# Layer-0 variance of a graph network from channel sums of h and h², in four column tiles of TensorE, in place of transposes and bn_stats

## The chip, the core and the metric

One core of a Trainium2 chip runs the kernel. Its engines work side by side, each through its own queue in order: TensorE (PE, with its weight loads PEld), VectorE (DVE), ScalarE (ACT), GpSimd (POOL) and SyncE (SP), which issues most of the DMAs. The metric is the device time of one execution in microseconds; less is better.

## The reference

128 graphs of 64 nodes with 128 channels each; every pair of nodes passes a message through a three-layer perceptron with two layer norms, the adjacency matrix masks the messages, their sum over j goes with the node through a second such perceptron, and the result is added to the node. Cut to what matters:

```python
def _layernorm(x, g, b):
    mu = jnp.mean(x, axis=-1, keepdims=True)
    var = jnp.mean(jnp.square(x - mu), axis=-1, keepdims=True)
    return (x - mu) * jax.lax.rsqrt(var + EPS) * g + b

def _mlp(x, w0, b0, g0, be0, w1, b1, g1, be1, w2, b2):
    h = jax.nn.relu(x @ w0 + b0)
    h = _layernorm(h, g0, be0)
    h = jax.nn.relu(h @ w1 + b1)
    h = _layernorm(h, g1, be1)
    return h @ w2 + b2

pair_feats = jnp.concatenate([f_i, f_j], axis=-1)
messages = _mlp(pair_feats, ...) * coupling_matrix[..., None]
agg = jnp.sum(messages, axis=2)
updated = part_feats + _mlp(jnp.concatenate([part_feats, agg], axis=-1), ...)
```

All inputs and the output are f32. About one pair in eight is an edge, so most messages are zero after the mask.

## The kernel before, in words

The kernel computes the messages of the edges alone. Each graph's edges are packed into 640 slots, five tiles of 128. A **chunk** is four tiles (512 slots), a **quad** is four graphs (five chunks, 20 tiles), a **block** is eight graphs (ten chunks), taken as four pairs of graphs. There are 160 chunks, 32 quads and 16 blocks. If a graph has more edges than slots, or adj is not 0 or 1, a flag computed at the end starts a dense version of everything (`dense_graph`), which these inputs don't need.

One loop runs over `n`, and in each iteration different chunks stand at different stages:

- `marks(n)`: products of edge counts (`tp`) and positions (`qs`) into the PSUM tile `mk`; DVE compares them with `cmpt` and gets the selection `s` of sending and receiving node for each slot.
- `layer0(n - 1)`: TensorE picks and adds the node terms (`abl`, `abh`, an exact split in two f32r parts) into `hps`; ACT makes `h` = relu(hps + b0), channels on partitions and edges along the row.
- `stats0(n - 2)`: the variance of `h` over its channels is needed for each edge. TensorE transposes the four tiles of `h` into the PSUM tile `hT`, and DVE takes `bn_stats` of each. After a quad's fifth chunk `std0_of` makes the standard deviation `SD`: `square_sum` joins the two halves that bn_stats gives with three operations on POOL and one on DVE, then come a step on DVE and a root on ACT.
- `layer1(n - L1)`, L1 = 9: POOL spreads `b1b` times the deviation into `sdb`; TensorE multiplies `h` with the weights `w1c`, which hold gain and centring, into `z`; DVE makes `y` = relu(z + sdb). So the division by the deviation is put off, since relu commutes with a positive factor.
- `stats1`: bn_stats of `y`, and after a quad `rstd1_of` makes the factor `Q`, with the same `square_sum`.
- `weights` and `reduce`, from iteration LW = 15 on: `w` = mask times `Q`; products of `w` and `y` summed by node into `ys`, two graphs in two column tiles of 64.

Two helpers run a step an iteration beside it: `prepare_block` for the next block (scan `rk` of adj, its counts `cum` and `deg`, the positions `pos`, then `xT` and the node terms by `w0a` and `w0b` in two column tiles) and `update_block` for the finished one (the second perceptron, with the same `std0_of` and `rstd1_of`).

A scheduler of the language sets the final order on each engine; on the chip each queue then runs strictly in that order. PSUM has eight banks: one each for `mk`, `hps`, `hT` and `ys`, two for `z`, and two (`bank()`) shared by all others. In the profile an f32 matmul shows as two instructions, one for each of its two passes.

Of the kernel before, what the change touches and what calls it, by code (L numbers as in the profile page):

```python
# [18 lines left out]
EPS = 1e-5  # L19
# [4 lines left out]
def tile_gnn(  # L24
# [36 lines left out]


    nc = tc.nc
    B, N, C = x.shape
# [11 lines left out]
    NB = NP // PB  # L76
    CPB = NCHK // NB

    xf = x.rearrange("b n c -> (b n) c")
# [17 lines left out]
    def row(ap, name, eng=nc.scalar):  # L97
# [4 lines left out]
    ones_row = const.tile([1, P], F32, name="ones_row")  # L102
    nc.vector.memset(ones_row, 1.0)
    mean_m = const.tile([P, P], F32, name="mean_m")
    nc.vector.memset(mean_m, 1.0 / C)
# [28 lines left out]
    first = const.tile([P, PB, 2, N], F32, name="first")  # L134
    nc.vector.memset(first, 1.0)
    nc.vector.memset(first[:, :, :, 0:1], 0.0)

# [20 lines left out]
    cumall = const.tile([P, NP], F32, name="cumall")  # L158
    nball = const.tile([P, NP // 8], F32, name="nball")
    W = {}  # L160
# [75 lines left out]
    def square_sum(stp, st, n, name):  # L236

        d = stp.tile([P, n], F32, name=name + "_d")
        s = stp.tile([P, n], F32, name=name + "_s")
        nc.gpsimd.tensor_tensor(d, st[:, :, 1], st[:, :, 4], op=ALU.subtract)  # L240
        nc.gpsimd.tensor_tensor(d, d, d, op=ALU.mult)  # L241
        nc.gpsimd.tensor_tensor(s, st[:, :, 2], st[:, :, 5], op=ALU.add)
        m2 = stp.tile([P, n], F32, name=name)
        nc.vector.scalar_tensor_tensor(m2, d, C / 4.0, s, op0=ALU.mult, op1=ALU.add)  # L244
        return m2

    def std0_of(stp, st, n, name):
        m2 = square_sum(stp, st, n, name)
        v = stp.tile([P, n], F32, name=name + "_v")
        nc.vector.tensor_scalar(v, m2, 1.0 / C, EPS, op0=ALU.mult, op1=ALU.add)  # L250
        sd = stp.tile([P, n], F32, name=name + "_sd")
        nc.scalar.activation(sd, v, AF.Sqrt)
        return v, sd

    def rstd1_of(stp, st, v0, n, name):
        m2 = square_sum(stp, st, n, name)
        v = stp.tile([P, n], F32, name=name + "_v")
        nc.vector.scalar_tensor_tensor(v, v0, EPS * C, m2, op0=ALU.mult, op1=ALU.add)
        sq = stp.tile([P, n], F32, name=name + "_sq")
        nc.scalar.activation(sq, v, AF.Sqrt, scale=1.0 / C)  # L260
        q = stp.tile([P, n], F32, name=name + "_q")
        nc.vector.reciprocal(q, sq)
        return q


    with ExitStack() as es:
# [4 lines left out]
        sp = es.enter_context(tc.tile_pool(name="sp", bufs=3))  # L271
        hp = es.enter_context(tc.tile_pool(name="hp", bufs=11))
        yp = es.enter_context(tc.tile_pool(name="yp", bufs=12))
# [5 lines left out]
        ps_h = es.enter_context(tc.tile_pool(name="ps_h", bufs=1, space=PSUM))  # L279
        ps_t = es.enter_context(tc.tile_pool(name="ps_t", bufs=1, space=PSUM))  # L280
        ps_z = es.enter_context(tc.tile_pool(name="ps_z", bufs=2, space=PSUM))
# [3 lines left out]
        def bank():  # L285
            return ps_m.tile([P, 512], F32, name="ms")
# [4 lines left out]
        def load_block(b):  # L291
            xn = blkp.tile([P, PB, C], F32, name="xn")
            nc.sync.dma_start(xn, xf[b * PB * P:(b + 1) * PB * P, :]
                              .rearrange("(q p) c -> p q c", p=P))
            an = blkp.tile([P, PB, N], F32, name="an")
            nc.sync.dma_start(an, adjp[:, b * PB:(b + 1) * PB, :])
            blocks[b] = {"xn": xn, "an": an}

        def prepare_block(b):
# [7 lines left out]
                out=rk.rearrange("p q j -> p (q j)"),  # L307
                data0=first[:, 0:PB // 2].rearrange("p a b j -> p (a b j)"), data1=anf,
# [5 lines left out]
            nc.vector.tensor_copy(deg, rk[:, :, N - 1])  # L314
            blk["deg"] = deg
# [22 lines left out]
            blk["qs"] = qs  # L338
            nc.vector.tensor_reduce(nball[:, b // 2:b // 2 + 1] if b % 2 else
                                    blknb, a2.rearrange("p q j -> p (q j)"),  # L340
                                    axis=AX.X, op=ALU.max, apply_absolute_value=True)
            if b % 2:
                nc.vector.tensor_tensor(nball[:, b // 2:b // 2 + 1],
                                        nball[:, b // 2:b // 2 + 1], blknb, op=ALU.max)
            yield
# [8 lines left out]
            for half in range(2):  # L354
                ps = bank()
                for k in range(4):
                    s = slice((4 * half + k) * N, (4 * half + k + 1) * N)
                    nc.tensor.matmul(ps[0:N, k * C:(k + 1) * C], lhsT=xT[:, s], rhs=w0a,  # L358
                                     start=True, stop=True)
                    nc.tensor.matmul(ps[N:P, k * C:(k + 1) * C], lhsT=xT[:, s], rhs=w0b,  # L360
                                     start=True, stop=True)

                hi = blkp.tile([P, 4, C], F32R, name="abh", bufs=6)
                lo = blkp.tile([P, 4, C], F32R, name="abl", bufs=6)
# [6 lines left out]
        blknb = const.tile([P, 1], F32, name="blknb")  # L371

# [5 lines left out]

        S, H, ST0, V0, SD, Y, ST1, Q, WT, YS = ({} for _ in range(10))

# [23 lines left out]
        def layer0(n):  # L404
# [8 lines left out]
            nc.scalar.activation(h, ps, AF.Relu, bias=b0c)  # L413
            H[n] = h

        def stats0(n):
            q, c = divmod(n, QC)
            ps = ps_t.tile([P, CH, P], F32, name="hT")
            for t in range(CH):
                nc.tensor.transpose(ps[:, t, :], H[n][:, t * P:(t + 1) * P], ident)  # L420
            if c == 0:
                ST0[q] = stp.tile([P, QT, 6], F32, name="st0")
            for t in range(CH):
                nc.vector.bn_stats(ST0[q][:, CH * c + t, :], ps[:, t, :])  # L424

        def layer1(n):
            q, c = divmod(n, QC)
            sdb = sbp.tile([P, CH, C], F32, name="sdb")
            nc.gpsimd.tensor_tensor(  # L429
                sdb, bc(W["b1b"], CH),  # L430
                SD[q][:, CH * c:CH * c + CH].unsqueeze(2).to_broadcast([P, CH, C]), op=ALU.mult)
            ps = ps_z.tile([P, CH, C], F32, name="z")
# [119 lines left out]

        L0, LS, L1 = 1, 2, QC + 4
        LW = L1 + QC + 1
# [10 lines left out]
        for n in range(end):  # L565
# [6 lines left out]
            if 0 <= n - L0 < NCHK:  # L572
                layer0(n - L0)
            if 0 <= n - LS < NCHK:
                stats0(n - LS)
                if (n - LS) % QC == QC - 1:
                    q = (n - LS) // QC
                    V0[q], SD[q] = std0_of(stp, ST0.pop(q), QT, "m20")
            if 0 <= n - L1 < NCHK:
                layer1(n - L1)  # L580
                stats1(n - L1)
                if (n - L1) % QC == QC - 1:
                    q = (n - L1) // QC
                    Q[q] = rstd1_of(stp, ST1.pop(q), V0.pop(q), QT, "m21")
            q, c = divmod(n - LW, QC)
# [15 lines left out]

        fl = const.tile([P, 2], F32, name="fl")
        nc.vector.tensor_reduce(fl[:, 0:1], cumall, axis=AX.X, op=ALU.max)
# [3 lines left out]
        ps = bank()  # L607
        nc.tensor.transpose(ps[0:2, 0:P], fl, ident)
        f2 = const.tile([2, 1], F32, name="f2")
        nc.vector.tensor_reduce(f2, ps[0:2, 0:P], axis=AX.X, op=ALU.max)  # L610
        ps = bank()
        nc.tensor.matmul(ps[0:1, 0:1], lhsT=f2, rhs=mean_m[0:2, 0:1], start=True, stop=True)
        flag = const.tile([1, 1], I32, name="flag")
# [122 lines left out]

    over = nc.values_load(flag[0:1, 0:1], min_val=0, max_val=2)
    with tc.If(over > 0):
# [36 lines left out]
```

## Time and profile before

| | |
|---|---|
| Median of 3 runs | 771.95 us (771.48 to 772.86) |
| Profiled execution | 771.45 us, span 769.7 us |
| ScalarE: relu of layer 0 | 160 of 688 ns |
| VectorE: bn_stats of layer 0 / of layer 1 | 640 of 283 ns / 640 of 278 ns |
| VectorE: s, y | 160 of 684 ns, 160 of 676 ns |
| TensorE: transposes of h | 640 of 288 ns |

A row of the profile names the line of the kernel, the engine, the operation, the tiles as out<-in, the shapes and the count, then busy time in us, the mean length of one in ns, and the engine's idle time before these with what ended most of it. The rows of a timeline begin with the start and the length in us. Lengths overlap: an engine begins the next instruction before the last is through, so the time that an instruction holds its queue is read from the starts of two neighbours.

### The profile page before, as it was taken

The page shows a single profiled execution, that of the slowest core. Times are in us where ns is not written, and L with a number is a line of the kernel's source. Part 1 is how long each engine was busy: PE and PEld are TensorE (multiplying, and loading weights), DVE is VectorE, ACT ScalarE, POOL GpSimd, SP SyncE. Part 2 cuts the span into 40 slices and gives each one's busy share as a digit, 9 for nine tenths or more (in the row PEclk, how much of TensorE's full clock was granted, in tenths as well). Part 3 has the DMA queues.
Part 4 walks back from the last instruction along what each step waited for, and adds up shares of the span by engine and source line. Part 5 has one row for each costly group of instructions (what it writes and reads, how often), then busy time and mean ns, then how long its engine had stood idle before and what let it go on. Part 6 is the DMA issues. An engine that isn't in the chain of part 4 may idle for free.

```text
span 769.7 us, 15357 instructions
## 1 busy us (share of the span) xinstructions
PE 654.7 (85%) x5667; PEld 558.6 (73%) x5667; DVE 673.4 (87%) x2397; ACT 208.0 (27%) x402; POOL 366.1 (48%) x651
## 2 busy tenths in 40 slices
PE   2688899898898979889898988889799898989773
PEld 2567778687777868778786877778687787878663
DVE  7678998988888999898998989989989898999872
ACT  1143232232232223223322323222232233222111
POOL 6346345444354454545455454545545354435531
PEclk9699999999899999999999999989999999999997
DMA  5000000100001010000101000010000000000000
GB/s 137 1 21 8 3 8 1 35 1 24 12 2 36 1 30 7 15 22 1 35 3 35 1 17 14 1 29 1 29 1 16 1 1 14 1 15 2 14 15 16
DMA packets 27883, 12.04 MB, mean 16 GB/s; under 512 B 10391, under 2 KB 27805, under 8 KB 27805
## 3 DMA queue, kind: packets, MB, share of 16 engines
q1 hardware_dynamic: 26496, 11.01, 5.1%
q8 instruction: 46, 0.75, 0.4%
q14 instruction: 33, 0.26, 0.1%
q10 hardware_dynamic: 1308, 0.01, 0.1%
HBM read 6.82 MB, written 4.19 MB: 14 GB/s over the span
## 4 chain that ended last, share of the span: by engine, by line
PE 48%; DVE 36%; POOL 10%; issue 2%; ACT 2%; DMA 1%; ACTq 0%; POOLq 0%; DVEq 0%
PE z L435 8%; PE ys L476 7%; DVE st L446 7%; PE ms L504 7%; PE hps L410 7%; DVE s L401 7%; PE hT L420 5%; DVE st L424 5%; PE mk L396 4%; PE ms L358 3%; DVE y L234 3%; POOL xo L488 3%; PE ms L494 2%; DVE uo L538 2%; POOL sdb L429 2%
## 5 line engine op out<-in xcount | busy, mean ns | idle before, releaser
L429 POOL TENSOR_TENSOR sdb<-b1b,m_sd 128x512 f32<-128x512 f32 x160 | 168.1, 1052 | 194.4 <-DVE y L234 136.0
L435 PE MATMUL z<-w1c,h 128*128 128x128 f32 x1280 | 201.3, 288 | 2.9 <-DVE y L234 2.5
L413 ACT ACTIVATE h<-hps,b0c 128x512 f32<-128x512 f32 x160 | 110.1, 688 | 311.8 <-PE hps L410 308.4
L435 PEld LDWEIGHTS z<-w1c,h 128*128 128x128 f32 x1280 | 173.4, 197 | 16.0 <-DVE y L234 7.6
L424 DVE BATCH_NORM_STATS2 st<-hT 128x6 f32<-128x128 f32 x640 | 147.4, 283 | 4.1 <-PE hT L420 3.9
L446 DVE BATCH_NORM_STATS2 st<-y 128x6 f32<-128x128 f32 x640 | 137.4, 278 | 0.0
L401 DVE TENSOR_TENSOR s<-mk,cmpt 128x512 fp32r<-128x512 f32 x160 | 109.4, 684 | 15.9 <-PE mk L396 14.8
L410 PE MATMUL hps<-s,abl 128*128 128x512 f32 (+3 forms) x256 | 101.9, 408 | 18.1 <-DVE s L401 17.7
L420 PE MATMUL hT<-ident,h 128*128 128x128 f32 x640 | 104.8, 288 | 6.6 <-DVE st L424 6.2
L234 DVE CUSTOM_DVE_ANT_0 y<-z,sdb 128x512 f32<-128x512 f32 x160 | 107.9, 676 | 1.3 <-POOL sdb L429 1.3
L396 PE MATMUL mk<-tp,qs 128*128 128x512 f16 (+3 forms) x256 | 66.4, 312 | 38.6 <-DVE s L401 30.1
L420 PEld LDWEIGHTS hT<-ident,h 128*128 128x128 f32 x640 | 75.2, 146 | 24.3 <-DVE st L424 18.7
L476 PE MATMUL ys<-y,w 128*64 128x128 f32 x1280 | 91.0, 281 | 1.8 <-DVE w L461 1.8
L476 PEld LDWEIGHTS ys<-y,w 128*64 128x64 f32 x1280 | 73.2, 139 | 14.9 <-issue 10.2
L410 PE MATMUL hps<-s,abh 128*128 128x512 f32 (+3 forms) x256 | 81.8, 336 | 0.0
L410 PEld LDWEIGHTS hps<-s,abl 128*128 128x128 f32 x256 | 51.6, 202 | 26.8 <-DVE s L401 20.2
L396 PEld LDWEIGHTS <-qs 128*128 128x128 f16 x256 | 25.1, 100 | 58.8 <-issue 57.0
L461 DVE TENSOR_TENSOR w<-ms,m_q 128x512 f32<-128x512 f32 (+1 forms) x128 | 61.0, 479 | 0.4 <-PE ms L456 0.4
L410 PEld LDWEIGHTS hps<-s,abh 128*128 128x128 f32 x256 | 52.0, 203 | 0.9
L240 POOL TENSOR_TENSOR m_d<-st 128x20 f32<-128x20 f32 x64 | 15.9, 248 | 73.8 <-DVE st L424 52.1
L244 DVE SCALAR_TENSOR_TENSOR m<-m_d,m_s 128x20 f32<-128x20 f32 x64 | 11.5, 179 | 32.0 <-POOL m_d L241 29.9
L488 POOL TENSOR_TENSOR xo<-xn,cu2b 128x512 f32<-128x512 f32 x16 | 20.5, 1282 | 34.3 <-DVE uo L538 33.3
(162 smaller groups left out, 939.1 us busy)
## 6 DMA issues: line engine op xcount, KB each, us to landing
xn<-in_x_dram SPq DMA_DIRECT2D x16, 256.0 KB, 2.8
out_dram<-uo SPq DMA_DIRECT2D x16, 256.0 KB, 2.3
an<-in_adj_dram SPq DMA_DIRECT2D x16, 128.0 KB, 2.2
w<-in_L_gnn_msg_w_dram SPq DMA_DIRECT2D x2, 64.0 KB, 2.3
u<-in_L_gnn_upd_w_dram SPq DMA_DIRECT2D x2, 64.0 KB, 2.1
w0a<-in_L_gnn_msg_w_dram SPq DMA_DIRECT2D x1, 64.0 KB, 1.8
w0b<-in_L_gnn_msg_w_dram SPq DMA_DIRECT2D x1, 64.0 KB, 2.4
u0a<-in_L_gnn_upd_w_dram SPq DMA_DIRECT2D x1, 64.0 KB, 2.3
```

The lines of the kernel that those rows point to most:

```text
L234: nc.vector._custom_dve(TENSOR_ADD_SAT, out=o, in0=ps, in1=sb, s0=BIG, s1=0.0)
L396: nc.tensor.matmul(ps[:, at:at + w], lhsT=blocks[g // (2 * PB)]["qs"][:, g // 2 % PB, g % 2, :], rhs=TP[g // 2][:, e:e + w], start=True, s ...
L401: nc.vector.tensor_tensor(s, ps, cmpt[:, o:o + CH * P], op=ALU.is_equal)
L410: nc.tensor.matmul(ps[:, at:at + w], lhsT=ab[:, g % 4, :], rhs=s[:, at:at + w], start=(k == 0), stop=(k == 1))
L413: nc.scalar.activation(h, ps, AF.Relu, bias=b0c)
L420: nc.tensor.transpose(ps[:, t, :], H[n][:, t * P:(t + 1) * P], ident)
L424: nc.vector.bn_stats(ST0[q][:, CH * c + t, :], ps[:, t, :])
L429: nc.gpsimd.tensor_tensor(sdb, bc(W["b1b"], CH), SD[q][:, CH * c:CH * c + CH].unsqueeze(2).to_broadcast([P, CH, C]), op=ALU.mult)
L435: nc.tensor.matmul(ps[:, t, :], lhsT=h[:, t * P:(t + 1) * P], rhs=W["w1c"], start=True, stop=True)
L446: nc.vector.bn_stats(ST1[q][:, CH * c + t, :], Y[n][:, t, :])
L461: nc.vector.tensor_tensor(w[:, t0:t1], ps[:, 0:nt * P].rearrange("p (t g m) -> p t g m", t=nt, g=2), qv[:, t0:t1].unsqueeze(3).to_broadcas ...
L476: nc.tensor.matmul(YS[b][g * N:(g + 1) * N, k, :], lhsT=w[:, t, g, :], rhs=y, start=(t == 0), stop=(t == TG - 1))
```

## The change

The layer-0 variance is computed as mean(h²) - mean(h)². ACT also squares `h` into `h2`. On every second chunk `sums(n)` has four products on TensorE: `h` and `h2` of this chunk and of the one before, each against `rowsel`, a 128x32 matrix that has 1/128 in one column and zeros elsewhere. Each product writes its own 32 partitions of one PSUM bank, `sm`, so the four stand in the four column tiles of 32. Two such groups add up in one bank. After four chunks (a batch, SB = 4) ACT copies the bank out (`sums_out`), TensorE transposes it in four pieces (`stats0(b)`), and DVE copies the means out, squares, subtracts; ACT takes the root.

Besides: the three small operations of `square_sum` go from POOL to DVE; EPS goes into the bias of the roots; `deg` and `cum` are copied by ACT and not by DVE; `nball` has a column for each block; `cmpt` is f16; `h` has 10 buffers instead of 11, `an` 3 instead of 5, the node terms 5 instead of 6; L1 is 8 instead of 9; and the flag at the end also asks whether the subtraction may have lost accuracy (mean² more than 16 times the variance).

```diff
+    rowsel = const.tile([P, 2, 32], F32, name="rowsel")
+    nc.vector.memset(rowsel, 0.0)
+    for r in range(2):
+        nc.vector.memset(rowsel[:, r, r:r + 1], 1.0 / C)
...
-    cmpt = const.tile([P, 4 * CAP], F32, name="cmpt")
+    cmpt = const.tile([P, 4 * CAP], F16, name="cmpt")
...
-        nc.gpsimd.tensor_tensor(d, st[:, :, 1], st[:, :, 4], op=ALU.subtract)
-        nc.gpsimd.tensor_tensor(d, d, d, op=ALU.mult)
-        nc.gpsimd.tensor_tensor(s, st[:, :, 2], st[:, :, 5], op=ALU.add)
+        nc.vector.tensor_tensor(d, st[:, :, 1], st[:, :, 4], op=ALU.subtract)
+        nc.vector.tensor_tensor(s, st[:, :, 2], st[:, :, 5], op=ALU.add)
+        nc.vector.tensor_tensor(d, d, d, op=ALU.mult)
...
-            nc.vector.tensor_copy(cum, ps[:, 0:PB])
+            nc.scalar.copy(cum, ps[:, 0:PB])
             deg = blkp.tile([P, PB], F32, name="deg", bufs=5)
-            nc.vector.tensor_copy(deg, rk[:, :, N - 1])
+            nc.scalar.copy(deg, rk[:, :, N - 1])
...
             nc.scalar.activation(h, ps, AF.Relu, bias=b0c)
             H[n] = h
-
-        def stats0(n):
-            q, c = divmod(n, QC)
-            ps = ps_t.tile([P, CH, P], F32, name="hT")
+            h2 = h2p.tile([P, CH * P], F32, name="h2")
+            nc.scalar.activation(h2, h, AF.Square)
+            H2[n] = h2
+
+        def sums(n):
+
+            b, c = divmod(n - 1, SB)
+            if c == 0:
+                SM[b] = ps_s.tile([P, CH * P], F32, name="sm")
+            for k, src in enumerate((H[n - 1], H2.pop(n - 1), H[n], H2.pop(n))):
+                nc.tensor.matmul(SM[b][32 * k:32 * k + 32, :], lhsT=rowsel[:, c // 2, :], rhs=src,
+                                 start=(c == 0), stop=(c == SB - 2))
+
+        def sums_out(b):
+            t = smp.tile([P, CH * P], F32, name="sums")
+            nc.scalar.copy(t, SM.pop(b))
+            SM[b] = t
+
+        def stats0(b):
+
+            src = SM.pop(b)
+            ps = bank()
             for t in range(CH):
-                nc.tensor.transpose(ps[:, t, :], H[n][:, t * P:(t + 1) * P], ident)
-            if c == 0:
-                ST0[q] = stp.tile([P, QT, 6], F32, name="st0")
-            for t in range(CH):
-                nc.vector.bn_stats(ST0[q][:, CH * c + t, :], ps[:, t, :])
+                nc.tensor.transpose(ps[:, t * P:(t + 1) * P], src[:, t * P:(t + 1) * P], ident)
+
+            v = ps.rearrange("p (t o k r) -> p k r o t", t=CH, o=2, k=2)
+            mm = stp.tile([P, 2, SB // 2, 2, CH], F32, name="mm")
+            for k in range(2):
+                nc.vector.tensor_copy(mm[:, k], v[:, k, 0:SB // 2])
+            mf = mm.rearrange("p k r o t -> p k (r o t)")
+            s = slice(b * SB * CH, (b + 1) * SB * CH)
+            nc.vector.tensor_tensor(msq[:, s], mf[:, 0], mf[:, 0], op=ALU.mult)
+            nc.vector.tensor_tensor(var0[:, s], mf[:, 1], msq[:, s], op=ALU.subtract)
+            sd = stp.tile([P, SB * CH], F32, name="sd")
+            nc.scalar.activation(sd, var0[:, s], AF.Sqrt, bias=eps_c)
+            SD[b] = sd
...
-        L0, LS, L1 = 1, 2, QC + 4
+        L0, LS, LT = 1, 2, 3
+        L1 = LT + SB + 1
...
-            if 0 <= n - LS < NCHK:
-                stats0(n - LS)
-                if (n - LS) % QC == QC - 1:
-                    q = (n - LS) // QC
-                    V0[q], SD[q] = std0_of(stp, ST0.pop(q), QT, "m20")
+            if 0 <= n - LS < NCHK and (n - LS) % 2:
+                sums(n - LS)
+                if (n - LS) % SB == SB - 1:
+                    sums_out((n - LS) // SB)
+            if 0 <= n - LT < NCHK and (n - LT) % SB == SB - 1:
+                stats0((n - LT) // SB)
```

The scheduler places the new operations. On TensorE before, in the middle of the program, the four transposes of a chunk (hT) stand between its layer 0 (hps) and an older chunk's layer 1 (z):

```order
L410 MATMUL hps<-s,abl 128x512
L410 MATMUL hps<-s,abh 128x512
L420 MATMUL hT<-ident,h 128x128 x4
L435 MATMUL z<-w1c,h 128x128 x2
L396 LDWEIGHTS qs
L396 MATMUL mk<-tp,qs 128x512
L435 MATMUL z<-w1c,h 128x128 x2
```

On TensorE now, a group of sums that stayed whole, on every second chunk (32x512 is its output; the inputs are h and h2 of two chunks):

```order
L420 MATMUL hps<-s,abl 128x384
L420 MATMUL hps<-s,abh 128x384
L420 MATMUL hps<-s,abl 128x128
L420 MATMUL hps<-s,abh 128x128
L435 MATMUL sm<-h,rowsel 32x512
L435 MATMUL sm<-h_2064,rowsel 32x512
L435 MATMUL sm<-h,rowsel 32x512
L435 MATMUL sm<-h_2132,rowsel 32x512
L471 MATMUL z<-w1c,h 128x128 x4
```

Four full-width transposes are gone from each chunk, and four products 32 wide stand there on every second one. In 47 of the 80 groups they stand so. In the other 33 the first product is torn off, as here on TensorE a little earlier, by transposes of the update (uh):

```order
L420 MATMUL hps<-s,abl 128x384
L420 MATMUL hps<-s,abh 128x384
L435 MATMUL sm<-h,rowsel 32x512
L530 MATMUL ms<-ident,uh 128x128 x4
L435 MATMUL sm<-h_1937,rowsel 32x512
L435 MATMUL sm<-h,rowsel 32x512
L435 MATMUL sm<-h_2007,rowsel 32x512
L471 MATMUL z<-w1c,h 128x128 x4
L512 MATMUL ys<-y,w 64x128 x10
```

So a full-width matmul now stands between two narrow stretches. Over the whole program (the dense version in it) TensorE goes between full-width and narrow outputs, or between widths of 64 and 32, 373 times, where it was 201.

On VectorE before, in an iteration with an update, ISA is the custom operation that makes y or uh, and m and um are small statistics that come from POOL:

```order
L244 SCALAR_TENSOR_TENSOR m_2714<-m_d,m_s 128x20
L376 TENSOR_SCALAR tp<-slot,cumall 128x640
L250 TENSOR_SCALAR m_v<-m_2714 128x20
L446 BN_STATS st_2602<-y 128x6 x4
L234 ISA uh<-ms,m_2622 128x512
L401 TENSOR_TENSOR s<-mk,cmpt 128x512
L511 BN_STATS ust_2755<-uh 128x6 x4
L424 BN_STATS st_2779<-hT 128x6 x4
L234 ISA y<-z,sdb 128x512
```

On VectorE now, around the four small operations of a batch (mm, msq, var) and the three that came from POOL (m_d, m_s, m_d):

```order
L453 COPY mm<-ms 128x16 x2
L456 TENSOR_TENSOR msq<-mm 128x16
L248 ISA y<-z,sdb 128x512
L457 TENSOR_TENSOR var_148<-mm,msq 128x16
L386 TENSOR_SCALAR tp<-slot,cumall 128x640
L482 BN_STATS st_2155<-y 128x6 x4
L411 TENSOR_TENSOR s<-mk,cmpt 128x512
L254 TENSOR_TENSOR m_d<-st_2155 128x20
L255 TENSOR_TENSOR m_s<-st_2155 128x20
L386 TENSOR_SCALAR tp<-slot,cumall 128x640
L256 TENSOR_TENSOR m_d<-m_d 128x20
```

The layer-0 bn_stats are gone from the queue, and the small statistics no longer leave it for POOL.

More of the change, by code (lines that the diff above doesn't have):

```diff
@@ L133, in tile_gnn @@
     nc.vector.memset(cmpt[0:N, :], 1.0)
-    first = const.tile([P, PB, 2, N], F32, name="first")
+    first = const.tile([P, PB, N], F32, name="first")
     nc.vector.memset(first, 1.0)
-    nc.vector.memset(first[:, :, :, 0:1], 0.0)
+    nc.vector.memset(first[:, :, 0:1], 0.0)
     w0a = mat(mw0[0:C, :], "w0a")
@@ L158, in tile_gnn @@
     cumall = const.tile([P, NP], F32, name="cumall")
-    nball = const.tile([P, NP // 8], F32, name="nball")
+    nball = const.tile([P, NB], F32, name="nball")
+    msq = const.tile([P, NCHK * CH], F32, name="msq")
+    var0 = const.tile([P, NCHK * CH], F32, name="var0")
     W = {}
@@ L377, in make_tp @@
             TP[p] = tp
-        S, H, ST0, V0, SD, Y, ST1, Q, WT, YS = ({} for _ in range(10))
+        S, H, H2, SM, SD, Y, ST1, Q, WT, YS = ({} for _ in range(10))
         def pieces(n):
@@ L607, in tile_gnn @@
         ps = bank()
-        nc.tensor.transpose(ps[0:2, 0:P], fl, ident)
-        f2 = const.tile([2, 1], F32, name="f2")
-        nc.vector.tensor_reduce(f2, ps[0:2, 0:P], axis=AX.X, op=ALU.max)
+        nc.tensor.transpose(ps[0:4, 0:P], fl, ident)
+        f2 = const.tile([4, 1], F32, name="f2")
+        nc.vector.tensor_reduce(f2, ps[0:4, 0:P], axis=AX.X, op=ALU.max)
         ps = bank()
-        nc.tensor.matmul(ps[0:1, 0:1], lhsT=f2, rhs=mean_m[0:2, 0:1], start=True, stop=True)
+        nc.tensor.matmul(ps[0:1, 0:1], lhsT=f2, rhs=mean_m[0:4, 0:1], start=True, stop=True)
         flag = const.tile([1, 1], I32, name="flag")
```

53 lines of the change are left out of this document (29 added, 24 removed).

## The prediction

> **What bounds the kernel now.** The page comes first, then the same engines in the steady part.
>
> ```profile
> span 769.7 us, 15357 instructions
> PE 654.7 (85%) x5667; PEld 558.6 (73%) x5667; DVE 673.4 (87%) x2397; ACT 208.0 (27%) x402; POOL 366.1 (48%) x651
> ```
>
> VectorE and TensorE are both nearly full, which the shares alone don't rank. So I cut the run into stages. The 16 blocks (four graph pairs, ten chunks each) are marked by one matmul, L333, that runs once a block:
>
> ```profile
> 107.06 0.60 PE L333 MATMUL ms<-pos,dq 128*128 128x256 f32 x2
> ...
> 648.02 0.60 PE L333 MATMUL ms<-pos,dq 128*128 128x256 f32 x2
> ```
>
> Twelve blocks lie between, so the period is (648.02 - 107.06) / 12 = 45.1 us. The busy times of just that stretch (columns: length, then PE, PEld, DVE, ACT, POOL, then the granted clock), and below it two shorter pieces of it:
>
> ```profile
> 107.06:648.02 540.96, 481.32 (x4226) 413.83 (x4225) 491.32 (x1771) 154.05 (x300) 264.55 (x467) 0.96 0.05 14
> 188.66:233.00 44.34, 39.12 (x328) 33.28 (x325) 38.14 (x138) 12.83 (x25) 20.57 (x38) 0.92 0.06 16
> 277.30:321.60 44.30, 39.08 (x355) 33.23 (x354) 41.28 (x151) 12.89 (x26) 22.65 (x40) 1.00 0.06 16
> ```
>
> Per block: DVE 40.9 us, PE 40.1, POOL 22.0, ACT 12.8, of 45.1. Which of the two waits for the other is told by the waits of the same stretch (us in all, times, longest):
>
> ```profile
> DVE m L244 <- POOL m_d L241: 24.5, 37, 1.2
> PE mk L396 <- DVE s L401: 23.9, 34, 0.8
> PE hps L410 <- DVE s L401: 16.5, 12, 1.5
> DVE s L401 <- PE mk L396: 12.0, 7, 2.9
> PE mk L396 <- DVE tp L376: 6.8, 12, 0.6
> ```
>
> PE waits for DVE in 47.2 us of these rows; DVE waits for PE in 12.0. DVE's largest wait is for POOL: the small statistics go DVE, POOL, DVE, and DVE stands still for 24.5 / 12 = 2.0 us a block. So DVE sets the end, with PE only 0.8 us a block less busy. Whatever is taken from DVE and put on PE meets that second limit at once.
>
> **DVE, part by part.** The change takes away the layer-0 bn_stats (st<-hT) and adds small operations.
>
> ```profile
> 352.73 0.88 DVE L424 BATCH_NORM_STATS2 st<-hT 128x6 f32<-128x128 f32 x4
> 353.52 0.68 DVE L234 CUSTOM_DVE_ANT_0 y<-z,sdb 128x512 f32<-128x512 f32 x1
> ```
>
> Four of them hold the queue from 352.73 to 353.52, 0.79 us (0.88 is their overlapping length). Ten chunks a block: -7.9.
>
> ```profile
> L314 DVE COPY deg<-rk 128x4 f32<-128x4 f32 x16 | 10.3, 644 | 0.0
> L244 DVE SCALAR_TENSOR_TENSOR m<-m_d,m_s 128x20 f32<-128x20 f32 x64 | 11.5, 179 | 32.0 <-POOL m_d L241 29.9
> L244 DVE SCALAR_TENSOR_TENSOR um<-um_d,um_s 128x4 f32<-128x4 f32 x32 | 5.0, 156 | 2.1 <-POOL um_d L241 2.1
> ```
>
> The deg copy goes to ACT: -0.6. Two layer-0 small operations on each of two quads go: 4 x 0.18 = -0.7. New are, a block, 6 operations for the two layer-1 quads, 6 for the update and 10 for 2.5 batches of layer-0 sums (two copies, a product, a subtraction). No row shows these; the nearest are 0.156 and 0.179 us, and the deg row (0.644, a four-element copy) is the far end. I take 0.16, so 22 x 0.16 = +3.5; at 0.644 it would be +14.2. Sum: -5.7, so DVE needs 35.2 us a block, and the 2.0 us of waiting for POOL goes with the POOL steps. Only at the far end (45.9) would DVE still bind. What is late next is PE.
>
> **PE, part by part**, over the whole run.
>
> ```profile
> L420 PE MATMUL hT<-ident,h 128*128 128x128 f32 x640 | 104.8, 288 | 6.6 <-DVE st L424 6.2
> 353.97 0.60 PE L420 MATMUL hT<-ident,h 128*128 128x128 f32 x4
> 354.41 0.83 PE L435 MATMUL z<-w1c,h 128*128 128x128 f32 x6
> 355.08 0.60 PE L494 MATMUL ms<-ident,uh 128*128 128x128 f32 x4
> 355.61 1.31 PE L476 MATMUL ys<-y,w 128*64 128x128 f32 x20
> 356.85 1.16 PE L504 MATMUL ms<-u1c,uhT 128*128 128x128 f32 x8
> 357.85 0.38 PE L396 MATMUL mk<-tp,qs 128*128 128x512 f16 x1
> ```
>
> Transposes: four start at 353.97 and the next matmul at 354.41, so 0.11 each. 640 go (-70.4); 40 batches bring 4 each (+17.6).
>
> The 80 groups of column-sum products. An f32 product is two passes (the count of two a product in L333), and a pass of 256 columns takes 0.60 - 0.38 = 0.22 us:
>
> ```profile
> L333 PE MATMUL ms<-pos,dq x32: 379/382/794, 14.5 to 648.2; 128*128 128x256 f32 x32
> ```
>
> So 512 columns are 0.44 a pass, 0.87 us a product alone. Do four column tiles run at once? The trace has two:
>
> ```profile
> 345.60 0.32 PE L358 MATMUL ms<-w0a,xT 128*64 128x128 f32 x1
> 345.61 0.32 PE L360 MATMUL ms<-w0b,xT 128*64 128x128 f32 x1
> 345.76 0.27 PE L358 MATMUL ms<-w0a,xT 128*64 128x128 f32 x1
> 345.77 0.27 PE L360 MATMUL ms<-w0b,xT 128*64 128x128 f32 x1
> ...
> 346.42 0.27 PE L358 MATMUL ms<-w0a,xT 128*64 128x128 f32 x1
> 346.42 0.27 PE L360 MATMUL ms<-w0b,xT 128*64 128x128 f32 x1
> ```
>
> Two different streams start together and the pair repeats every 0.11, the time of one full-width pass: two tiles cost what one does. Four are not shown. Bounds for a group: 0.44 (were a narrow pass to stream at twice the rate) to 3.48 (one after another). I take 0.87, four at once, since the nearest row overlaps fully: 80 x 0.87 = +69.6.
>
> In the program's order 33 of the 80 groups are torn: the first product stands alone, then other matmuls, then the other three. The lone one overlaps nothing: +33 x 0.87 = +28.7.
>
> Every change between full-width and narrow matmuls costs. Above, the transposes from 355.08 should end at 355.52 but ys starts at 355.61 (0.09); ys's ten pairs need 1.09 of 1.24 (0.15); u1c's eight passes need 0.89 of 1.00 (0.11). That is 0.35 for a round trip. The order has 373 changes after and 201 before, 86 round trips more: +30.
>
> Sum for PE: -70.4 + 17.6 + 69.6 + 28.7 + 30 = +75.5 us, 4.7 a block. PE goes from 40.1 to 44.8, DVE from 40.9 to 35.2: the bound moves to PE, at about the old period.
>
> The Trainium skill, "TensorE: Matmul & The Clock Gate", section "Part 3: Packing small matmuls — row/col tiling", gives 2.38 times for three column tiles of 512 columns, not 3; at that efficiency a group would take 1.26 times a lone product, an estimate, +18 us in all and 775 us in place of 757. The two-tile rows show no such loss, and no run here shows three or four.
>
> **Hidden parts.** ACT gains a square a chunk and a copy of the sums every four:
>
> ```profile
> L413 ACT ACTIVATE h<-hps,b0c 128x512 f32<-128x512 f32 x160 | 110.1, 688 | 311.8 <-PE hps L410 308.4
> L429 POOL TENSOR_TENSOR sdb<-b1b,m_sd 128x512 f32<-128x512 f32 x160 | 168.1, 1052 | 194.4 <-DVE y L234 136.0
> ```
>
> At 0.69 each, 12.5 a block are 8.6; ACT goes to 21.4 of 45 and waits for PE's layer 0 most of its time, so this costs nothing while a square ends within the iteration between its layer 0 and its sums. Were that cover gone, each fourth product would wait up to 0.69, 80 x 0.69 = 55 us. POOL loses small steps and its sdb is unchanged. The layer-0 deviations now have two iterations (9 us) before their use instead of three; sums copy 0.69, four transposes 0.60, four DVE steps 0.64 and one sdb 1.05 are 3.0 and a root, so some 6 us are left for queueing. The pipeline is one iteration shorter, worth 0 to 4.5 us at the end; I take 2.
>
> **The sum.** Per block: 44.8 for PE. Off this goes part of the slow clock: it stands at 0.96, and a mean of 0.04 below full is 0.04 x 45 = 1.8 us; a piece at 0.92 and one at 1.00 stand above with like work. These dips need idle PE, and I let half go (-0.9). On it come PE's waits that stay: of 47.2 / 12 = 3.9 us I keep a tenth, 0.4, because DVE now has 9 us to spare. Period 44.3, and 16 x (45.1 - 44.3) = 12.8 less, with the shorter end 14.8. The profiled execution took 771.45 us (span 769.7), so 756.7; the median of the runs is 0.5 higher: 757.
>
> **Rivals.**
> 1. More gain: PE never starves, so clock dips and waits both go: 44.8 - 1.8 = 43.0, less the pipeline tails after each wait inside "busy" (0.27 us long less the 0.11 it holds the queue, 0.16, times five), 42.2: 46 us less, 725. For it: PE's idle time is nearly all DVE's doing. Against: 640 transposes are replaced by work in which PE still depends on single PSUM banks. The skill's same page, section "Part 4: PE-mode transpose", says transposes don't count as activity for the clock; by that rule the dips would go with them and this rival's 725 is the time. The piece at 1.00 above ran with all its transposes, which does not bear it out. Chance 0.10.
> 2. Slower, by PE's in-order queue: the place is the 33 torn groups and their switches, which make PE full; it decides from 0.3 us of waiting a block (44.8 + 0.3 = 45.1) if the clock stays at 0.96. With 1.5 us, a third of today's: 46.3, +19, 790. Chance 0.20.
> 3. The products overlap only two at a time: each of 80 groups takes 0.87 more, +70: 827. Chance 0.13. One after another: 47 whole groups x 3 and 33 torn ones x 2 are 207 x 0.87 = +180: 937. Chance 0.04. Here the change doesn't do what its four tiles say.
> 4. Both limits meet and nothing moves: 0.06.
>
> **Chances.** The forecast (742 to 768) has 0.47. Faster by over 0.2%, the least that this kernel's runs can tell from no change: 0.47 + 0.10 = 0.57; within it 0.06; slower 0.20 + 0.13 + 0.04 = 0.37. The range reaches from just above rival 1 to rival 3: 730 to 828.
>
> **What would show it.** Right: sm products in fours that start within 0.05 us and hold PE about 0.9; PE busier than DVE; DVE's rows of waiting for POOL's m_d gone; DVE rows of waiting for PE (s for mk, y for z) grown to several us a block. Wrong: a stagger of 0.4 or more inside a whole group (rival 3); PE's clock unchanged with PE waiting over 1 us a block for DVE, ACT or sdb (rival 2); new two-input DVE steps far above 0.16.

## The result, and the profile after

The changed kernel takes 743.36 us (median of 4 runs, 741.81 to 745.39) against 771.92 us before: 0.963 times the time, 95% interval 0.960 to 0.966. It is 28.6 us faster, where 15 were forecast; 743.36 lies in the range of 730 to 828, near the fast end of the forecast (742 to 768), 13.6 us below the predicted 757.

The page of the changed kernel, first the span and the busy times, then the chain that ended last (here by engine):

```profile
span 743.3 us, 15105 instructions
PE 678.8 (91%) x5827; PEld 504.9 (68%) x5827; DVE 619.9 (83%) x1998; ACT 335.3 (45%) x642; POOL 311.5 (42%) x363
...
PE 54%; DVE 33%; POOL 5%; DMA 3%; issue 2%; ACT 1%; SPq 0%; DVEq 0%; ACTq 0%; POOLq 0%
```

PE and DVE have changed places: PE is now the fuller one. Its share of the chain was 48% before and is 54% now, so the chain alone doesn't tell that the limit moved. The same block marker as before (now L349), from the timeline of PE:

```profile
95.97 0.70 PE L349 MATMUL ms<-pos,dq 128*128 128x256 f32 x2
...
618.05 0.70 PE L349 MATMUL ms<-pos,dq 128*128 128x256 f32 x2
```

That is (618.05 - 95.97) / 12 = 43.5 us a block, 1.57 less than before. The busy times of these twelve blocks and of the two pieces ahead of them (length, then PE, PEld, DVE, ACT, POOL, granted clock):

```profile
95.97:618.05 522.08, 498.93 (x4346) 372.29 (x4345) 451.96 (x1464) 248.84 (x479) 225.75 (x254) 0.99 0.05 15
...
0.00:58.00 58.00, 39.73 (x258) 26.27 (x259) 38.64 (x95) 24.47 (x46) 29.85 (x51) 1.00 0.20 49
58.00:95.97 37.97, 36.02 (x327) 26.39 (x325) 32.52 (x105) 19.18 (x36) 16.22 (x22) 1.00 0.02 5
```

The same of the kernel before, at its start:

```profile
0.00:58.00 58.00, 35.24 (x210) 28.04 (x210) 40.69 (x102) 13.85 (x22) 28.57 (x52) 0.85 0.21 53
58.00:107.06 49.06, 41.82 (x353) 34.75 (x352) 44.98 (x164) 13.00 (x24) 24.18 (x44) 1.00 0.02 4
```

The span is 26.4 us shorter, and the markers say where: twelve blocks at 1.57 are 18.9 us; the fourth block's marker comes 11.1 us earlier (95.97 against 107.06), with the clock at 1.00 in the first 58 us instead of 0.85; and the end behind the last marker is 3.6 us longer (125.3 against 121.7). Per block PE is busy 41.6 us, DVE 37.7, ACT 20.7, POOL 18.8.

The waits of the twelve blocks (us in all, times, longest):

```profile
DVE y L248 <- PE z L471: 33.9, 31, 1.4
DVE abl L379 <- ACT abh L378: 20.6, 23, 2.1
...
PE mk L406 <- DVE s L411: 9.7, 17, 1.1
...
DVE uh L248 <- PE ms L540: 8.0, 12, 0.7
```

DVE's waits for POOL (m_d) are gone, PE's waits for `s` have shrunk from 23.9 and 16.5 us to 9.7, and DVE now waits for PE's `z`.

The groups of four products, from PE's timeline, one whole (eight instructions are four products of two passes) and one torn:

```profile
309.00 0.39 PE L420 MATMUL hps<-s,abh 128*128 128x512 f32 x1
309.32 1.06 PE L435 MATMUL sm<-h,rowsel 128*32 128x512 f32 x8
310.31 1.16 PE L471 MATMUL z<-w1c,h 128*128 128x128 f32 x8
311.31 0.44 PE L492 MATMUL ms<-pick,tp 128*128 128x128 f16 x5
...
323.13 1.05 PE L435 MATMUL sm<-h,rowsel 128*32 128x512 f32 x2
324.11 0.32 PE L370 MATMUL ms<-w0a,xT 128*64 128x128 f32 x1
...
325.72 1.06 PE L435 MATMUL sm<-h,rowsel 128*32 128x512 f32 x6
326.71 1.16 PE L471 MATMUL z<-w1c,h 128*128 128x128 f32 x8
```

Read from start to start: four products together hold PE for 0.99 us, one alone for 0.98, three for 0.99. So the four column tiles run at once, and a torn group costs twice what a whole one does. Over the run 47 groups are whole (median 0.996) and 33 torn (0.976 and 0.989), as the order showed.

The full-width neighbours of a group pay too. In the kernel before, the same two stand beside each other:

```profile
339.25 0.40 PE L410 MATMUL hps<-s,abh 128*128 128x512 f32 x1
339.49 1.05 PE L435 MATMUL z<-w1c,h 128*128 128x128 f32 x8
340.38 0.28 PE L456 MATMUL ms<-pick,tp 128*128 128x128 f16 x2
```

There hps holds PE 0.24 us and eight passes of z 0.89. Around a group it is 0.32 (309.00 to 309.32) and 1.00 (310.31 to 311.31). With the 0.12 by which a group's 0.99 exceeds the 0.87 of one product alone, a round trip between the widths costs some 0.3 us.

DVE's small operations by shape, of the whole run (count, then busy us, mean ns):

```profile
L456 DVE TENSOR_TENSOR msq<-mm 128x16 f32<-128x16 f32 x40 | 23.2, 580 | 0.0
...
L255 DVE TENSOR_TENSOR m_s<-st 128x20 f32<-128x20 f32 x32 | 16.3, 510 | 0.0
...
L254 DVE TENSOR_TENSOR um_d<-ust 128x4 f32<-128x4 f32 x32 | 11.7, 366 | 0.1
...
L457 DVE TENSOR_TENSOR var<-mm,msq 128x16 f32<-128x16 f32 x40 | 6.5, 162 | 0.0
```

The last row is what was expected of all of them; the first three are two to four times that. All nine new groups come to 101 us, 6.3 a block instead of 3.5.

### The profile page after: what moved, and what is told of

Same layout as the page of the kernel before. It is cut to its first block, busy times and chain, and to the rows that moved or that the text cites. A ratio compares the mean times of both kernels' runs of the same rounds, so it can differ in the third digit from the quotient of the medians.

```text
span 743.3 us, 15105 instructions
## 1 busy us (share of the span) xinstructions
PE 678.8 (91%) x5827; PEld 504.9 (68%) x5827; DVE 619.9 (83%) x1998; ACT 335.3 (45%) x642; POOL 311.5 (42%) x363
## 4 chain that ended last, share of the span: by engine, by line
PE 54%; DVE 33%; POOL 5%; DMA 3%; issue 2%; ACT 1%; SPq 0%; DVEq 0%; ACTq 0%; POOLq 0%
PE z L471 10%; PE sm L435 10%; PE ms L540 8%; PE ys L512 7%; DVE y L248 6%; PE hps L420 6%; DVE st L482 5%; DVE s L411 5%; PE ms L370 4%; PE mk L406 3%; PE ms L530 3%; DVE w L497 3%; DMA an<-in_adj_dram 2%; POOL sdb L465 2%; DVE ust L547 2%
## 5 line engine op out<-in xcount | busy, mean ns | idle before, releaser
L465 POOL TENSOR_TENSOR sdb<-b1b,sd 128x512 f32<-128x512 f32 x160 | 166.3, 1052 | 158.9 <-ACT sd L459 83.4
L471 PEld LDWEIGHTS z<-w1c,h 128*128 128x128 f32 x1280 | 159.9, 191 | 69.7 <-issue 64.7
L471 PE MATMUL z<-w1c,h 128*128 128x128 f32 x1280 | 182.9, 282 | 2.6 <-DVE y L248 2.6
L248 DVE CUSTOM_DVE_ANT_0 y<-z,sdb 128x512 f32<-128x512 f32 x160 | 108.9, 681 | 46.5 <-PE z L471 44.3
L435 PE MATMUL sm<-h,rowsel 128*32 128x512 f32 x640 | 121.3, 607 | 0.0
L426 ACT ACTIVATE h<-h 128x512 f32<-128x512 f32 x160 | 100.7, 629 | 4.0
L512 PE MATMUL ys<-y,w 128*64 128x128 f32 x1280 | 84.7, 279 | 0.7 <-DVE w L497 0.7
L520 POOL TENSOR_TENSOR m<-c2u,deg 128x512 f32<-128x512 f32 x16 | 16.6, 1040 | 98.8 <-DVE uh L248 89.8
L378 ACT CAST abh<-ms 128x512 fp32r<-128x512 f32 x32 | 18.7, 585 | 55.5 <-PE ms L372 55.5
L379 DVE TENSOR_TENSOR abl<-ms,abh 128x512 fp32r<-128x512 f32 x32 | 22.1, 691 | 24.0 <-ACT abh L378 23.7
L370 PEld LDWEIGHTS ms<-w0a,xT 128*64 128x64 f32 x256 | 29.9, 144 | 15.1 <-DVE w L497 11.7
```

The lines of the kernel that those rows point to most:

```text
L248: nc.vector._custom_dve(TENSOR_ADD_SAT, out=o, in0=ps, in1=sb, s0=BIG, s1=0.0)
L426: nc.scalar.activation(h2, h, AF.Square)
L435: nc.tensor.matmul(SM[b][32 * k:32 * k + 32, :], lhsT=rowsel[:, c // 2, :], rhs=src, start=(c == 0), stop=(c == SB - 2))
L465: nc.gpsimd.tensor_tensor(sdb, bc(W["b1b"], CH), SD[b][:, CH * c:CH * c + CH].unsqueeze(2).to_broadcast([P, CH, C]), op=ALU.mult)
L471: nc.tensor.matmul(ps[:, t, :], lhsT=h[:, t * P:(t + 1) * P], rhs=W["w1c"], start=True, stop=True)
L512: nc.tensor.matmul(YS[b][g * N:(g + 1) * N, k, :], lhsT=w[:, t, g, :], rhs=y, start=(t == 0), stop=(t == TG - 1))
```

## The experiments

**The theory** after the result: before, DVE set the pace (its work and its wait for POOL), and PE's busy time overstated what PE needed; the change takes DVE's work away, so PE's torn groups become the next thing that costs. **Rivals:** the gain comes from the small statistics that left POOL; or PE had been the limit all along and gained by the clock; or a torn group is hidden anyway.

### 1 and 2. The small statistics alone, and the change without them

In the kernel before, the three operations of `square_sum` go to VectorE (first run); in the changed kernel they go back to POOL (second run, the same edit the other way):

```diff
-        nc.gpsimd.tensor_tensor(d, st[:, :, 1], st[:, :, 4], op=ALU.subtract)
-        nc.gpsimd.tensor_tensor(d, d, d, op=ALU.mult)
-        nc.gpsimd.tensor_tensor(s, st[:, :, 2], st[:, :, 5], op=ALU.add)
+        nc.vector.tensor_tensor(d, st[:, :, 1], st[:, :, 4], op=ALU.subtract)
+        nc.vector.tensor_tensor(s, st[:, :, 2], st[:, :, 5], op=ALU.add)
+        nc.vector.tensor_tensor(d, d, d, op=ALU.mult)
```

> The kernel before, with only the three small statistics operations of square_sum moved from POOL to DVE (six places a block, so 18 operations). My theory (DVE sets the end before, and the gain of the change is the bn_stats that leave it): DVE loses 2.0 us a block of waiting for POOL and gains 18 x 0.16 = 2.9 us of work, so about +0.9 us a block: 772 to 790 us, granted clock still near 0.956. Rival (the gain comes mainly from ending the handoffs between DVE and POOL): 745 to 760 us.

> The changed kernel, with only the small statistics put back on POOL. My theory (PE sets the end after, DVE has 5.8 us a block to spare): the handoffs return to DVE's queue but fall into its slack, 742 to 750 us. Rival (handoffs matter): 2.0 us a block or more come back, 775 us or more.

Measured: 797.97 us, 1.034 times before (1.030 to 1.038), and 742.5 us, 0.961 (0.957 to 0.965), the changed kernel's own time. The windows of the first between its markers:

```profile
111.10:672.10 561.00, 500.74 (x4226) 430.34 (x4225) 515.49 (x1982) 153.99 (x300) 224.53 (x251) 0.92 0.05 13
```

The first run is slower than its theory's 772 to 790 us, and its clock fell to 0.92 where 0.956 was expected; the rival, a gain, is out. DVE goes to 515.49 / 12 = 43.0 us a block, 2.1 more than before, and the period to 46.75, 1.7 more. That fits DVE as the limit, with a wait for POOL that was cheaper than the work done by itself; alone it doesn't prove it, since PE's busy time also grew, by 1.6 us a block at the lower clock. In the second run, whose time the theory forecast, the wait is back:

```profile
DVE y L248 <- PE z L471: 24.3, 19, 1.5
...
DVE m L258 <- POOL m_d L255: 21.4, 18, 2.1
```

It is 21.4 us in place of part of the waiting for `z`, and the time is the same. In the changed kernel this part brought nothing: the 2.0 us a block of DVE's waiting that the prediction saw go were no gain. The other small changes that came along (`cmpt` in f16, fewer buffers, L1 = 8) were not tried apart; `s`, which reads `cmpt`, takes 680 ns where it took 684.

### 3. The groups kept whole by a critical section

The loop of the four products moves in under the section, otherwise unchanged:

```diff
+            with tc.tile_critical():
                 for k, src in enumerate((H[n - 1], H2.pop(n - 1), H[n], H2.pop(n))):
```

> The changed kernel, with the four products of a group kept together in PE's order (no group is torn; before 33 of 80 were). A lone product held PE 0.98 us with its switches. My theory (PE sets the end): 33 x 0.98 = 32 us less work on PE; most of it is gained, 712 to 724 us. Rival (DVE, busy 37.7 of 43.5 us a block, is the next limit close by, or PE's waits take its place): 733 us or more.

Measured: 796.89 us, 1.031 (1.027 to 1.035). A miss. The theory's 712 to 724 us did not come. All 80 groups are whole, but a row of the waits in its profiled execution (810 us) shows what the section costs:

```profile
PEld sm L436 <- issue: 95.3, 81, 3.0
```

Ahead of a group's weight load the queue of loads stands 95.3 / 81 = 1.2 us with nothing to wait for that the profile shows, and PE itself is idle ahead of each of the 80 groups for 1.0 us on the mean, 80 us in all, where 33 lone products of 0.98 were to be saved. So the run says nothing on the theory; run 5 reaches the same order without a section.

### 4. The square done twice on ACT

```diff
             nc.scalar.activation(h2, h, AF.Square)
+            nc.scalar.activation(h2, h, AF.Square)
```

> The changed kernel, with ACT's square of h done twice (the second overwrites the first): 160 x 0.63 = 101 us more on ACT, 27 of 43.5 us a block. My theory (ACT is covered): 742 to 750 us. Rival (PE waits for the squares, or the longer ACT queue delays the relu that frees the layer-0 bank): 0.63 us on every second chunk or more, 790 us or more.

Measured: 743.95 us, 0.965 (0.960 to 0.970), the changed kernel's time, with ACT at 26.5 us a block. As forecast, ACT's part is hidden, with room for one more square a chunk.

### 5. The four products written in the reverse order

```diff
-            for k, src in enumerate((H[n - 1], H2.pop(n - 1), H[n], H2.pop(n))):
+            for k, src in reversed(list(enumerate((H[n - 1], H2.pop(n - 1), H[n], H2.pop(n))))):
```

The product that is ready last (`h2` of this chunk) now stands first, so the scheduler has nothing to start early.

> The changed kernel, with the four products of a group written in the reverse order, so that the scheduler tears none of the 80 groups (33 were torn) and PE changes its width 309 times and not 373; nothing drains PE and no wait is added, as the section of e3 did. My theory (PE sets the end; a lone product holds it 0.98 us with its switches): 33 x 0.98 = 32 us less on PE, 712 to 726 us. Rival (DVE, 37.7 of 43.5 us a block, or a chain through ACT and POOL is the limit close by): 733 us or more.

Measured: 710.31 us, 0.921 (0.915 to 0.926), 33 us below the changed kernel. All 80 groups are whole in its trace. Its windows:

```profile
89.47:587.11 497.64, 469.90 (x4346) 368.49 (x4344) 450.90 (x1464) 247.16 (x479) 226.92 (x254) 1.00 0.06 16
```

PE is busy 39.2 us a block instead of 41.6, and the period is 41.5 instead of 43.5. A group that stays whole saves a lone product's 0.98 us and what its switches cost the neighbours, some 0.2: 33 x 1.17 = 39 us, which is also about what PE's busy time fell by (16 x 2.4 us). The gain is 33 us, a little more than was forecast: most of the loss of a torn group is paid, and it was in the result all the time. DVE's waits for `z` fall with it, from 33.9 us in the twelve blocks to 11.

### 6 and 7. The whole groups with a load on PE, and with one on DVE

Two of the four layer-1 products of each chunk are done twice (320 products of two passes of 0.11 us, 71 us, 4.4 a block); or two of its bn_stats (64 us, 4.0 a block):

```diff
-            for t in range(CH):
+            for t in (0, 0, 1, 1, 2, 3):
                 nc.tensor.matmul(ps[:, t, :], lhsT=h[:, t * P:(t + 1) * P], rhs=W["w1c"],
```

```diff
+            for t in range(2):
+                nc.vector.bn_stats(ST1[q][:, CH * c + t, :], Y[n][:, t, :])
```

> The kernel of e5 with two of the four layer-1 products of each chunk done twice: 160 x 4 passes x 0.11 = 71 us more on PE, all groups still whole. My theory (PE sets the end after the change): 55 us or more above e5. Rival (PE has room, something else sets the end): under 30 us above e5.

> The kernel of e5 with two more bn_stats of y a chunk (written over the same statistics): 320 x 0.2 = 64 us more on DVE (7 of 80 groups are torn in its order, 7 us). My theory (DVE has over 4 us a block to spare): under 35 us above e5, of which 7 are torn groups. Rival (DVE still sets the end): 60 us or more above e5.

Measured: 751.95 us (0.975, 0.968 to 0.982), 42 more than run 5 for 71 us of PE's work; and 745.8 us (0.967, 0.959 to 0.974), 35.5 more for 64 us of DVE's. In run 7 seven groups are torn again, some 7 of the 35.5 us. So each load costs about half of itself (42 of 71; 28 of 64), and neither theory's number came. The likely reading is that PE and DVE share the limit; each load also gives the scheduler another order, and that was not held apart.

### 8. The same PE load in the kernel before

> The kernel before with the same load on PE as in e6 (71 us of products). My theory (before, DVE sets the end and PE idles 5.0 us a block): 16 x 4.5 = 71 us of work fall mostly into 80 us of idle time, 780 to 805 us. Rival (PE set the end before already): 830 us or more.

Measured: 771.17 us against 771.14, ratio 1.003 (0.999 to 1.008). 71 us of work on PE cost nothing that can be told from zero, less than the theory's 780 to 805 us allowed. Its windows:

```profile
106.63:642.87 536.24, 504.19 (x4706) 452.69 (x4705) 489.35 (x1766) 151.57 (x300) 264.03 (x467) 1.00 0.05 14
```

PE's busy time grows by 1.9 us a block (42.0 against 40.1) for 4.4 of work, and the granted clock of the stretch goes from 0.96 to 1.00. PE was not the limit before: with its gaps filled, it needs at most 42.0 - 4.4 = 37.6 us a block, not 40.1. At most, because PE is still idle 2.7 us of a block in this run, so some of what counts as busy is waiting yet.

### 9. The same PE load in the changed kernel

> The changed kernel (32 of its groups torn) with the load of e6 on PE: two of four layer-1 products of each chunk done twice, 71 us of PE. Before, this load cost nothing (e8); in the kernel with whole groups 42 us (e6). My theory (in the changed kernel PE, busy 41.6 of 43.5 us a block, sets the end alone): 55 us or more above it, 798 us or more. Rival (DVE and PE share the limit there as in e6): 780 to 792 us.

Measured: 781.27 us, 1.009 (1.007 to 1.012), 38 more than the changed kernel, in the rival's range. (Runs 9 to 12 were made on another chip, where the kernel before took 773.64 us and not 771.14; by the ratios it is 36 more.) The load now costs about half of itself, where it was free before. The windows:

```profile
98.59:649.13 550.54, 543.15 (x4827) 424.54 (x4825) 453.24 (x1464) 250.45 (x480) 225.96 (x254) 1.00 0.05 14
```

PE is busy 45.3 of 45.9 us. Less the load, the changed kernel needs at most 40.9 us of PE a block, 3.3 more than run 8's 37.6 (both at a clock of 1.00). The 3.3 are the least that the change added, since PE is full here and was not in run 8. The remaining 2.6 of the changed kernel's 43.5 are gaps that the load first fills.

### 10. All products of the sums in one column tile

Each of the eight products of a batch has a selector with its column elsewhere, and all write partitions 0 to 31 (cut to the products; the copy and the transposes behind them take these 32 partitions alone):

```diff
-                nc.tensor.matmul(SM[b][32 * k:32 * k + 32, :], lhsT=rowsel[:, c // 2, :], rhs=src,
-                                 start=(c == 0), stop=(c == SB - 2))
+                nc.tensor.matmul(SM[b][0:32, :], lhsT=rowsel[:, 2 * k + c // 2, :], rhs=src,
+                                 start=(c == 0 and k == 0), stop=(c == SB - 2 and k == 3))
```

> The changed kernel with all products of the sums in one column tile (each source its own row of the same 32 partitions, one after another), so none overlaps. My theory (four tiles run at once, a group holds PE 0.87 us and not 3.5): 47 whole groups lose 3 x 0.87 and 33 torn ones 2 x 0.87, 180 us in all, 900 to 935 us. Rival (the tiles save little, since the streams share something, or PE has room): 800 us or less.

Measured: 884.65 us, 1.144 (1.140 to 1.148), 141 more than the changed kernel. PE's timeline has a lone product and its three others:

```profile
329.80 1.04 PE L435 MATMUL sm<-h,rowsel 128*32 128x512 f32 x2
...
332.38 2.76 PE L435 MATMUL sm<-h,rowsel 128*32 128x512 f32 x6
335.08 1.16 PE L473 MATMUL z<-w1c,h 128*128 128x128 f32 x8
```

Three products hold PE for 2.70 us (332.38 to 335.08) instead of 0.99, and a whole group 3.55 (median) instead of 0.996. The overlap of the column tiles is what makes the change pay; without it the kernel is slower than before by 111 us. The 141 fall short of the forecast 180 in two steps. PE is busy 10.2 us a block more (51.75 in the window between its markers, against 41.58), 163 us in all; and 1.7 of these fill gaps that the changed kernel had, so the period is 8.4 longer.

### 11 and 12. The whole groups with the small statistics on POOL

Run 5 with `square_sum` on POOL, as in run 2; then with `msq` and `var` there as well:

```diff
-            nc.vector.tensor_tensor(msq[:, s], mf[:, 0], mf[:, 0], op=ALU.mult)
-            nc.vector.tensor_tensor(var0[:, s], mf[:, 1], msq[:, s], op=ALU.subtract)
+            nc.gpsimd.tensor_tensor(msq[:, s], mf[:, 0], mf[:, 0], op=ALU.mult)
+            nc.gpsimd.tensor_tensor(var0[:, s], mf[:, 1], msq[:, s], op=ALU.subtract)
```

> The kernel of e5 (whole groups) with the three operations of square_sum back on POOL. DVE's two-input small operations take 0.20 to 0.51 us in the changed kernel's profile where I had put 0.16. My theory (with whole groups PE and DVE are both close to the end, and these operations wait for POOL's long ones on DVE's queue): DVE loses 1.4 us a block, about half of it shows, 692 to 706 us. Rival (the handoffs DVE, POOL, DVE cost as much as they free): 708 us or more.

> The kernel of e11 with the product and the subtraction of the layer-0 variance (msq, var) on POOL too. msq alone takes 0.58 us on DVE. My theory: another 1.8 us a block less on DVE, 2.5 x 0.4 us more on POOL, 686 to 702 us and not slower than e11. Rival (the layer-0 chain to sdb, now through POOL, becomes late): slower than e11 by 5 us or more.

Measured: 727.9 us (0.941, 0.935 to 0.946), 18 more than run 5, in the rival's range; and 701.31 us (0.906, 0.903 to 0.908), 9 less than run 5, as its theory had it, and the fastest of all. By the ratios, which take out the chip, it is 15 more and 12 less. Their windows, run 11 first:

```profile
89.94:603.33 513.39, 474.74 (x4346) 371.76 (x4344) 439.32 (x1320) 247.04 (x479) 249.52 (x398) 0.98 0.05 15
```

```profile
91.56:580.68 489.12, 466.96 (x4347) 366.46 (x4345) 408.74 (x1261) 246.00 (x479) 263.05 (x459) 1.00 0.06 16
```

DVE is busy 37.6 us a block in run 5, 36.6 in run 11 and 34.1 in run 12; the periods are 41.5, 42.8 and 40.8. So moving `square_sum` frees 1.0 us of DVE and costs 1.3, as in the rival: the handoff to POOL, free in run 2, counts here. That the torn groups hid it there is a guess that no run tests. Moving `msq` and `var` frees another 2.5 and brings 2.0. Why the second handoff is cheap and the first is not was not tried apart: the two steps also differ in the order on DVE's queue, so the price of a handoff is open.

## Why the prediction was right or wrong

**What bounds the kernel before: right.** DVE set the end. Run 8 shows that PE did not (71 us for nothing), and run 1 fits it from DVE's side (2.1 us a block more work, 1.7 longer). But "PE only 0.8 us a block less busy", so that DVE's work "meets that second limit at once", was wrong: PE had room for at least 4.4.

**PE's need: the step that was mis-sized.** "PE goes from 40.1 to 44.8" was wrong in its start. The 40.1 us were busy time of an engine that waits and is clocked down; with its gaps filled it needs at most 37.6 (run 8). The 4.7 that were added to it were nearly right. A round trip between the widths was taken at 0.35 us and costs some 0.3 (0.12 in the group, the rest at its two neighbours), so the 86 of them are 27 us instead of 30, and by its rows the change adds (-70.4 + 17.6 + 69.6 + 28.7 + 27) / 16 = 4.5 us a block; run 9 less run 8 gives 3.3, which is the least. After the change PE needs at most 40.9 us a block (run 9), not 44.8.

**Four tiles at once: right.** Four hold PE as long as one does (0.996 and 0.976), and run 10 prices the alternative. Rival 3 is out. The Trainium skill, "TensorE: Matmul & The Clock Gate", section "Part 3: Packing small matmuls — row/col tiling", gives 2.38 times for three column tiles of 512 columns. The trace shows more: three products take 2.70 us one after another (run 10) and 0.99 side by side, 2.7 times, and four 3.55 and 0.996, 3.6 times.

**The torn groups: right in mechanism and size.** 33 x 0.87 was forecast, with the switches counted apart; 33 x 0.98 were measured in the trace, switches at the neighbours not counted, and run 5 gains 33 us by removing them. Rival 2 named this place as what could make the kernel slower. It cost what it was said to cost, inside a gain that was larger than thought.

**DVE: the bn_stats went as forecast, the small operations were mis-sized.** 22 x 0.16 = 3.5 us a block were taken, 6.3 were measured, between the two bounds that were given (3.5 and 14.2). DVE is busy 37.7 us, not 35.2. Two-input steps far above 0.16 were one of the prediction's own signs of being wrong; DVE had room for them.

**"The bound moves to PE": half right.** PE leads the chain, but in runs 6, 7 and 9 a load on either engine costs about half of itself, as if PE and DVE shared the limit. That would also be why the period is 43.5 us and not PE's 40.9. The forecast kept 0.4 us of PE's waits and took 0.9 off for the clock; in truth 2.6 come on top of PE's need. The two errors, 3.9 us too much for PE's work and 3.1 too little for its gaps, nearly cancel, and 0.8 us a block was left of them. That 44.3 came out so near to 43.5 was luck.

**POOL's handoff: gone as forecast, and worth nothing.** Its 2.0 us a block vanished from the waits; with it put back the time is the same (run 2). The forecast's sum, which is PE's, did not count on it.

**The clock: under-estimated.** Half of the loss was to go; in the twelve blocks the clock went from 0.96 to 0.99, and in the first 58 us from 0.85 to 1.00. That first stretch goes with most of the 11.1 us by which the fourth marker comes earlier, where the forecast's 0.8 us a block gave 2.4. Which of the two, the clock or the shorter work of DVE, brought them was not tried apart. Rival 1 expected this rise, and that part of PE's "busy" is waiting, and gave 725 us for both. It also tied the rise to the transposes by the Trainium skill, "TensorE: Matmul & The Clock Gate", section "Part 4: PE-mode transpose", which says that the full clock doesn't engage for them, since they don't count as busy in the same way. Run 8 keeps all 640 of them and its clock rises the same, to 1.00 in the twelve blocks, so the rise needs no transpose to go; filling PE's gaps was enough. Whether a transpose counts is not decided by this.

**ACT and the deviations: right.** Hidden, even with the square twice (run 4); DVE waits only 1.3 us in the whole run for `sdb`, which holds the deviations. **The end:** 3.6 us longer, where 2 less were taken.

## What to carry to other kernels

The busy time of an engine that waits is an upper bound of its need: a load of known size, added in its place, lowers that bound and shows whether the engine sets the pace. When products share the array as column tiles, look in the final order for groups that the scheduler tears, and write the operand that is ready last first: that one line was worth more here than the change itself. When work leaves the limiting engine, price the next two limits, since they are likely to meet.

## What the runs showed of the hardware

**Small two-input operations on VectorE stretch beside GpSimd.** Two engines of the changed kernel at the same time, first DVE's timeline, then POOL's:

```profile
308.21 1.26 DVE L456 TENSOR_TENSOR msq<-mm 128x16 f32<-128x16 f32 x1
...
310.00 0.16 DVE L457 TENSOR_TENSOR var<-mm,msq 128x16 f32<-128x16 f32 x1
```

```profile
308.17 1.27 POOL L524 TENSOR_TENSOR xo<-xn,cu2b 128x512 f32<-128x512 f32 x1 [4.83 <-DVE mm L453]
```

`msq`, 16 elements, takes as long as POOL's operation beside it. Of its 40 instances 14 ran with POOL idle, 0.175 us each, and 26 with POOL at work, 0.80 on the mean. The one-input copies `mm` from PSUM show nothing of the kind (0.153 and 0.163). This agrees with the Trainium skill, "GPSIMD Engine Reference", section "1. Specifications", which says that POOL shares its SBUF interfaces with VectorE and that DVE instructions with two SBUF inputs contend. On POOL itself, in run 12, the same operation takes 0.22 us:

```profile
L456 POOL TENSOR_TENSOR msq<-mm 128x16 f32<-128x16 f32 x40 | 8.6, 216 | 30.2 <-DVE mm L453 30.2
```

**The clock stands higher where PE's gaps are filled, but not by PE's share alone.** Between the markers PE is busy 89% in the kernel before (clock 0.96) and in run 1 (0.92), 94% in run 8 and in run 5 (1.00), 99% in run 9 (1.00). The 71 us more work of run 8 raised the clock; the two clocks at 89% show that the share doesn't fix it.
